# Carried scan states written two rounds ahead, and small preparation products asked for one round earlier, in a four-layer conv, scan and attention network

## The chip, the cores and the metric

The kernel runs on one core of one Trainium2 chip. The metric is the device time of one execution in microseconds; the median of three runs is given. One core has a matrix engine (TensorE, PE in the profile; PEld are its weight loads), three engines for elementwise work (VectorE or DVE, ScalarE or ACT, GpSimd or POOL), and a queue for transfers (SyncE or SP). Each engine has its own stream of instructions, and they wait for each other where data or a buffer asks for it.

## What is computed

The input is an image batch x of 4 x 56 x 56 x 96. Four layers follow each other: layers 0 and 1 are selective scans over the 3136 pixels of an image in four directions (rows and columns, each forwards and backwards), layers 2 and 3 are linear attention with a quantized feed-forward network. The change touches only the scans. For one direction, with 192 channels d and 16 states s per channel, the reference does this:

```
dt  = softplus(dt_raw @ dtw + dtb)            # per pixel and channel
d_a = exp(dt * a)                             # a = -exp(A_log), per channel and state
d_b = dt * b_ssm
h   = d_a * h + d_b * x_t                     # over the pixels, one after another
y_t = sum over s of h * c_ssm
```

dt_raw, b_ssm and c_ssm are small projections of the pixel's 192 channels. So each of the 192 x 16 = 3072 states per image and direction has a recurrence along 3136 pixels.

## The kernel before

**Tiling of the scan.** A direction of an image is cut into 7 chunks of 448 pixels. In a chunk the 3072 states are handled in 8 rounds (two halves e of the channels, four quarters q of the states), each with three groups g of 128 partitions. This gives 2 layers x 4 images x 4 directions x 7 chunks x 8 rounds = 1792 rounds; they are one long loop, `scans`, and everything else is woven into it.

**A round n.** The tile h has for each of the three groups 448 columns and two spare ones. It goes through these steps:

- `begin(n)`: TensorE spreads b over the partitions into the single PSUM buffer b (`spread_b`, L593), and GpSimd writes d_b * x for the third group into h (L686).
- `products(n)`: VectorE writes the same for the groups 0 and 1 (L691), reading b.
- `carried(n)`: ScalarE copies the states at the end of the chunk before (tile carry, 128x3) into the spare columns of h (L662), one per group, where the scan starts: columns 1, 451 and 901 in a forward direction, 450, 900 and 1350 in a reversed one. It is left out in the first chunk of a direction.
- `scan(n, g)`: VectorE runs the recurrence over group g (L698), reading the decays da[g] from PSUM.
- `decay(n + 1, g)`: ScalarE writes the decays of the next round into da[g] (L652), which has one buffer per group, so it follows `scan(n, g)`.
- `kept(n)`: ScalarE copies the states at the end of h into carry (L667).
- Last, GpSimd multiplies h with c into hc (L739); two rounds later TensorE sums hc over the states into y (`add_up`, L770), and every fourth time ScalarE moves y to SBUF (L777).

The tile h has three buffers. hc of round n is the last reader of h of round n.

**The order of the work is written out by hand.** The engines' streams follow the order of the Python program. In the loop over n it is: products(n); preparation of later chunks (`prepare`); slot F, where other work (the "lanes": projections, convolutions, layer norms and attention of other images) issues its ScalarE instructions; `prepare_on_scalar`; filler products that keep TensorE active (`keep_busy`, L757); begin(n + 1); add_up; the projections of a later chunk (`ahead`); scan and decay of group 0, carried(n + 1); slot C, where the lanes issue their TensorE instructions; scan and decay of groups 1 and 2; hc. `spend` books what the round's ScalarE and TensorE work costs, and the lanes may only issue what fits the rest; the filler is what is missing to a fixed amount.

**The preparation of a chunk** runs from 14 rounds before its first one. o counts its rounds, negative ahead of the chunk. In o = -12 and -11 TensorE projects the pixels into the single PSUM buffer pp (L433); in -10 ScalarE copies them to the tile cf (`rows`); then the rounding error of cf's bf16 half is kept in its lower rows, in two steps: `less` subtracts on TensorE (L586), ScalarE copies the rest (L573). Then `step_size` makes dt on TensorE (L479) for each half of the channels, into pp again, and `softplus` takes it from there on ScalarE (L489, L491). In -5 GpSimd forms dt * x (`times_u`, L504), and transfers spread both over the partitions.

Of the kernel before, what the change touches and what calls it, by code (L numbers as in the profile page):

```python
# [11 lines left out]
F32 = mybir.dt.float32  # L12
# [22 lines left out]
WIDE = NG * ROW + 2  # L35
# [131 lines left out]
class Net:  # L167
# [368 lines left out]
    def prepare(self, ch, o):  # L536

        nc = self.nc  # L540
        if o == -14:
            self.parameters(ch)
        elif o == -12:
            self.inputs(ch)
        elif o == -9:
            ch.cd = self.dram.tile([2 * NS, CS], F32, tag="cd", name="cd", bufs=3)
            nc.sync.dma_start(ch.cd, ch.cf[: 2 * NS])
            self.less(ch, 64)
        elif o == -8:
            self.less(ch, 96)  # L550
        elif o in (-7, -6):
            self.step_size(ch, o + 7)
        elif o == -5:
            self.times_u(ch)
            ch.dtd = self.park(ch.dtc)
        elif o == -4:
            ch.dud = self.park(ch.duc)
            self.spread_dt(ch, 0)
        elif o == -3:
            self.spread_du(ch, 0)  # L560
        elif o == 0:
            self.spread_du(ch, 1)
            self.spread_dt(ch, 1)
        if -3 <= o <= 0:
            self.fetch(ch, o + 3)

    def prepare_on_scalar(self, ch, o):

        if o == -10:
            self.rows(ch)  # L570
        elif o in (-9, -8):
            part = slice(64 if o == -9 else 96, 128)
            self.nc.scalar.copy(ch.cf[part], ch.ps[part])  # L573
        elif o in (-7, -6):
            self.softplus(ch, o + 7)

    def projected(self, ch, o):

        return () if o not in (-12, -11) else (o + 12,) if not ch.first else (0, 1) if o == -11 else ()
# [20 lines left out]
    def scans(self):  # L600

        nc, sp = self.nc, self.sp
        chunks = []
        for l in range(2):  # L610
            for i in range(NB):
                for n, (orient, rev) in enumerate(ORDER[l]):
                    for step in range(NCS):
                        ch = Step()
                        ch.l, ch.i, ch.orient, ch.rev, ch.step = l, i, orient, rev, step
                        ch.k = 2 * orient + rev if l == 0 else orient + 2 * rev
                        ch.c = NCS - 1 - step if rev else step
                        ch.n, ch.first = n, n == 0 and step == 0
                        ch.skip = n == 0
                        ch.last = n == 3 and step == NCS - 1  # L620
                        ch.cb, ch.dt, ch.du = [], [], []
                        chunks.append(ch)
        rounds = [(ch, e, q) for ch in chunks for e in range(NE) for q in range(NQ)]
        per = NE * NQ


        da = [self.psum.tile([128, 512], F32, name=f"da{g}")[:, : CS + 4] for g in range(NG)]
        for t in da:
            nc.vector.memset(t, 0.0)

        def steps(n):

            return [(ch, n - per * j) for j, ch in enumerate(chunks[max(0, n // per) : n // per + 3], max(0, n // per))]

        def ahead(n, project):
            for ch, o in steps(n):
                for e in self.projected(ch, o):
                    project(ch, e)

        for n in range(-14, 0):  # L640
            for ch, o in steps(n):
                self.prepare(ch, o)
            for ch, o in steps(n):
                self.prepare_on_scalar(ch, o)
            ahead(n, self.project_step)


        def decay(n, g):

            if n < len(rounds):  # L650
                ch, e, q = rounds[n]
                nc.scalar.activation(da[g][:, INNER], ch.dt[e][:, g], AF.Exp, scale=ch.par.na[:, e, q, g : g + 1])  # L652

        def column(t, at):

            return t[:, at : at + 2 * ROW + 1 : ROW]

        def carried(n):

            if n < len(rounds) and rounds[n][0].step:  # L660
                ch, e, q = rounds[n]
                nc.scalar.copy(column(hs[n], ROW if ch.rev else 1), ch.par.carry[:, e, q])  # L662

        def kept(n):
            ch, e, q = rounds[n]
            if ch.step < NCS - 1:
                nc.scalar.copy(ch.par.carry[:, e, q], column(hs[n], 2 if ch.rev else CS + 1))  # L667

        def own(n):
            ch, e, q = rounds[n]  # L670
            return NQ * e + q in (OWN_TAIL if ch.l and ch.i else OWN)

        hs, bs = {}, {}

        def tokens(t):

            return self.groups(t, 2)[:, :, :CS]

        def begin(n):

            if n < len(rounds):
                ch, e, q = rounds[n]
                bs[n] = self.spread_b(ch, q)
                hs[n] = sp.tile([128, WIDE], F32, name="h", bufs=3)
                if not own(n):
                    nc.gpsimd.tensor_tensor(tokens(hs[n])[:, 2], ch.du[e][:, 2], ch.cb[q][:, 1], ALU.mult)  # L686

        def products(n):
            ch, e, q = rounds[n]
            for g in range(3 if own(n) else 2):  # L690
                nc.vector.tensor_tensor(tokens(hs[n])[:, g], ch.du[e][:, g], bs[n], ALU.mult)  # L691

        def scan(n, g):
            ch, e, q = rounds[n]
            c = 1 if ch.step else 0
            way = slice(CS + 1 + c, 1, -1) if ch.rev else slice(2 - c, CS + 2)
            h = hs[n][:, g * ROW :]
            nc.vector.tensor_tensor_scan(h[:, way], da[g][:, way], h[:, way], 0.0, ALU.mult, ALU.add)  # L698

        begin(0)  # L700
        self.exp_and_ln()
        self.tables = True
        for g in range(NG):
            decay(0, g)
        late = []
        for n, (ch, e, q) in enumerate(rounds):
            r = NQ * e + q
            products(n)
            for c, o in steps(n):
                self.prepare(c, o)  # L710
            self.half_round()
            strided = [1.5 + 1.5 * ch.orient] * (r % NQ == 2)
            ahead(n, lambda c, _: strided.append(1.5 + 1.5 * c.orient))
            self.spend((0.6, 0.7, 1.7, 0, 0, 0, 0.7, 0.6)[r], (0.4, 1.3, 1.3, 0, 0, 0, 0, 0.4)[r] + sum(strided))
            yield "F", n, r
            for c, o in steps(n):
                self.prepare_on_scalar(c, o)
            ended = late.pop(0) if len(late) == 2 else None
            if ended:
                self.keep_busy(ended[2])  # L720
            begin(n + 1)
            if ended:
                self.add_up(*ended)
            ahead(n, self.project_step)
            self.half_round()
            for g in range(NG):
                if g == 1:
                    yield "C", n, r
                if g == 2 and ended and ended[2] == NQ - 1:
                    self.spend(0.6, 0)  # L730
                    self.keep_sums(*ended[:3])
                scan(n, g)
                if g == 2:
                    kept(n)
                decay(n + 1, g)
                if g == 0:
                    carried(n + 1)
            hc = sp.tile([128, NG, CS], F32, name="hc", bufs=3)
            nc.gpsimd.tensor_tensor(  # L739
                hc, tokens(hs[n]), ch.cb[q][:, 0].unsqueeze(1).to_broadcast([128, NG, CS]), ALU.mult,  # L740
            )
            late.append((ch, e, q, hc))
            del hs[n], bs[n]
        for ended in late:
            self.add_up(*ended)
        self.keep_sums(ch, e, q)
        yield "C", len(rounds), 0
# [619 lines left out]
```

## Time and profile before

| | |
|---|---|
| median of 3 runs | 8560.88 us (8560.84 to 8582.3) |
| profiled execution | span 8573.6 us, granted TensorE clock 0.892 |
| first and last hc (L739) | 115.8 us, 8187.3 us |
| copy of carried states (L662) | 1536 times, median 195 ns |
| subtraction product (L586) | 448 times, median 380 ns |
| dt product (L479) | 448, recorded as 896 passes, median 612 ns |
| filler products (L757) | 5061 times, 1410.0 us |

A page of the profile begins with each engine's busy time, its share of the span and its number of instructions. The groups that follow are instructions of one line: what they write and read, shape, count; then their busy time in us and the mean duration in ns; and last the idle time of the engine just before them, with what ended most of it. The table of waits gives for each pair the total in us, how often, and the longest. In the order of time a line begins with the start in us and the duration; "[idle before <-releaser]" tells how long the engine had stood, and for whom. Idle time counts only on the engine that sets the pace.

### The profile page before, as it was taken

The page shows a single profiled execution, that of the slowest core. Times are in us where ns is not written, and L with a number is a line of the kernel's source. Part 1 is how long each engine was busy: PE and PEld are TensorE (multiplying, and loading weights), DVE is VectorE, ACT ScalarE, POOL GpSimd, SP SyncE. Part 2 cuts the span into 40 slices and gives each one's busy share as a digit, 9 for nine tenths or more (in the row PEclk, how much of TensorE's full clock was granted, in tenths as well). Part 3 has the DMA queues.
Part 4 walks back from the last instruction along what each step waited for, and adds up shares of the span by engine and source line. Part 5 has one row for each costly group of instructions (what it writes and reads, how often), then busy time and mean ns, then how long its engine had stood idle before and what let it go on. Part 6 is the DMA issues. An engine that isn't in the chain of part 4 may idle for free. (4 is left out here: it accounts for less than half of the span.)

```text
span 8573.6 us, 119867 instructions
## 1 busy us (share of the span) xinstructions
PE 7605.2 (89%) x33851; PEld 2757.7 (32%) x33851; DVE 7521.8 (88%) x9555; ACT 6085.3 (71%) x12807; POOL 7185.1 (84%) x3991
## 2 busy tenths in 40 slices
PE   7888888898889888898889989998899888998997
PEld 3333322232323223232222323333333233333355
DVE  5999999989998999989899999999999999999931
ACT  5777777776777767776677766677766777767746
POOL 4898898988988988889889898898988888888820
PEclk8888889898998988989899989988999889998986
DMA  5776776667766676666767777666766667666621
GB/s 154 175 178 176 189 187 173 167 160 180 179 167 160 170 183 172 168 167 162 183 171 175 173 182 171 164 162 169 190 168 155 160 173 186 166 164 158 171 61 45
DMA packets 944162, 1417.81 MB, mean 165 GB/s; under 512 B 169410, under 2 KB 936644, under 8 KB 942628
## 3 DMA queue, kind: packets, MB, share of 16 engines
q1 hardware_dynamic: 942720, 1408.34, 66.6%
q8 instruction: 266, 4.36, 0.2%
q14 instruction: 404, 3.31, 0.1%
q10 hardware_dynamic: 772, 1.80, 0.1%
HBM read 1141.42 MB, written 268.14 MB: 164 GB/s over the span
## 5 line engine op out<-in xcount | busy, mean ns | idle before, releaser
L739 POOL TENSOR_TENSOR hc<-h,cb 128x1344 f32<-128x1344 f32 x1792 | 4883.2, 2725 | 826.4 <-DVE h L698 601.0
L698 DVE TENSOR_TENSOR_SCAN h<-da,h 128x449 f32<-128x449 f32 (+1 forms) x5376 | 5502.3, 1071 | 44.8 <-POOL h L686 37.8
L652 ACT ACTIVATE da<-dt,na 128x448 f32<-128x448 f32 x5376 | 3389.6, 633 | 820.3 <-DVE h L698 697.0
L691 DVE TENSOR_TENSOR h<-du,b 128x448 f32<-128x448 f32 x3584 | 2039.9, 606 | 516.4 <-ACT h L662 407.9
L770 PE MATMUL y<-hc,four 128*32 128x448 f32 x14336 | 1945.1, 618 | 7.1 <-POOL hc L739 7.1
L686 POOL TENSOR_TENSOR h<-du,cb 128x448 f32<-128x448 f32 x1792 | 1752.9, 978 | 103.7 <-DMA cb<-cd 96.6
L757 PE MATMUL y<-w,zeros 128*96 128x448 bf16 x5061 | 1410.0, 399 | 0.0
L593 PE MATMUL b<-cf,sel 128*128 128x448 bf16 x1792 | 680.4, 380 | 788.3 <-DVE h L691 782.0
L757 PEld LDWEIGHTS <-zeros 128*96 128x96 bf16 x5061 | 618.2, 135 | 1158.4 <-issue 1005.0
L662 ACT COPY h<-carry 128x3 f32<-128x3 f32 x1536 | 290.2, 189 | 630.1 <-POOL h L686 620.9
L770 PEld LDWEIGHTS y<-hc,four 128*32 128x32 f32 x14336 | 295.8, 113 | 1274.5 <-issue 877.0
L433 PE MATMUL pp<-U,wd 96*128 96x448 f32 x896 | 684.1, 853 | 7.3 <-DMA U<-u 4.3
L766 PE MATMUL y<-Y,ident 96*96 96x448 f32 x672 | 543.9, 899 | 13.5 <-ACT carry L667 5.3
L914 PE MATMUL ps<-win,dg 64*64 64x220 f32 (+9 forms) x1944 | 520.1, 469 | 0.0
L504 POOL TENSOR_TENSOR duc<-dtc,U 96x896 f32<-96x896 f32 x224 | 482.3, 2153 | 4.5 <-ACT dtc L491 4.5
L479 PE MATMUL pp<-cf,wd 12*96 12x448 f32 (+1 forms) x896 | 468.1, 603 | 16.1 <-ACT dtc L489 13.3
L667 ACT COPY carry<-h 128x3 f32<-128x3 f32 x1536 | 295.0, 192 | 175.6 <-DVE h L698 172.4
L573 ACT COPY cf<-pp 64x448 f32<-64x448 f32 x448 | 235.6, 526 | 180.8 <-PE pp L586 172.1
L777 ACT COPY Y<-y 96x448 f32<-96x448 f32 x448 | 341.0, 761 | 26.3 <-PE y L770 25.5
L489 ACT ACTIVATE dtc<-pp,wd 96x448 f32<-96x448 f32 x448 | 280.5, 626 | 107.6 <-PE pp L479 102.4
L914 PEld LDWEIGHTS ps<-win,dg 64*64 64x64 f32 (+2 forms) x1944 | 231.9, 163 | 334.9 <-issue 295.2
L593 PEld LDWEIGHTS <-sel 128*128 128x128 bf16 x1792 | 181.8, 101 | 417.4 <-issue 352.5
(432 smaller groups left out, 5970.0 us busy)
## 6 DMA issues: line engine op xcount, KB each, us to landing
cb<-cd SPq DMA_DIRECT2D x3584, 112.0 KB, 3.8
dt<-dd SPq DMA_DIRECT2D x1792, 168.0 KB, 4.3
du<-dd SPq DMA_DIRECT2D x1792, 168.0 KB, 4.1
dd<-dtc SPq DMA_DIRECT2D x224, 336.0 KB, 3.0
dd<-duc SPq DMA_DIRECT2D x224, 336.0 KB, 3.1
U<-u SPq DMA_DIRECT2D x112, 168.0 KB, 4.8
z<-w SPq DMA_DIRECT2D x56, 224.0 KB, 4.3
u<-w SPq DMA_DIRECT2D x56, 224.0 KB, 4.0
```

The lines of the kernel that those rows point to most:

```text
L433: self.nc.tensor.matmul(ch.ps.rearrange("p (a b) -> p a b", b=HS), ch.par.wx[:, e], self.in_order(self.U[e], ch.orient, ch.c * CS, CS), st ...
L504: self.nc.gpsimd.tensor_tensor(in_rows(ch.duc), in_rows(ch.dtc), u[:, :, lo : lo + CS // HS], ALU.mult)
L593: self.nc.tensor.matmul(ps, self.sel[:, q], self.upper(ch.cf), start=True, stop=True)
L652: nc.scalar.activation(da[g][:, INNER], ch.dt[e][:, g], AF.Exp, scale=ch.par.na[:, e, q, g : g + 1])
L686: nc.gpsimd.tensor_tensor(tokens(hs[n])[:, 2], ch.du[e][:, 2], ch.cb[q][:, 1], ALU.mult)
L691: nc.vector.tensor_tensor(tokens(hs[n])[:, g], ch.du[e][:, g], bs[n], ALU.mult)
L698: nc.vector.tensor_tensor_scan(h[:, way], da[g][:, way], h[:, way], 0.0, ALU.mult, ALU.add)
L739: nc.gpsimd.tensor_tensor(hc, tokens(hs[n]), ch.cb[q][:, 0].unsqueeze(1).to_broadcast([128, NG, CS]), ALU.mult,)
L757: self.nc.tensor.matmul(self.y[:C], self.zeros, self.some, start=False, stop=False)
L766: nc.tensor.matmul(o, w, self.in_order(a, ch.orient, ch.c * CS, CS), start=True, stop=False)
L770: nc.tensor.matmul(self.y[32 * n : 32 * n + 32], self.four, hc[:, g], start=n == 3, stop=n == 3 or q == NQ - 1,)
L914: self.nc.tensor.matmul(o[:, a - r0 : e - r0, x0:x1], diag[:, tap], win[:, a + dy - lo : e + dy - lo, x0 + dx : x1 + dx], start=n == 0, st ...
```

## The change

Two parts of the hand-written order are moved. First, the tile h of round n + 2 is taken, and the carried states are copied into it, at the end of round n, after the last decay; before, the tile of round n + 1 was taken in `begin(n + 1)` and the copy came after the first decay of round n + 1, in the middle of the scans. So VectorE's products and GpSimd's product into the same tile come after the copy instead of before it. Second, TensorE's `less` and `step_size` are asked for one round earlier, at the end of the round's TensorE work beside the projections, so that they can be done when ScalarE comes to read them in the next round. The bookings in `spend` are moved by a round to match. No arithmetic changes.

```diff
@@ prepare
         elif o == -9:
             ch.cd = self.dram.tile([2 * NS, CS], F32, tag="cd", name="cd", bufs=3)
             nc.sync.dma_start(ch.cd, ch.cf[: 2 * NS])
-            self.less(ch, 64)
-        elif o == -8:
-            self.less(ch, 96)
-        elif o in (-7, -6):
-            self.step_size(ch, o + 7)
         elif o == -5:
...
+    def on_tensor(self, ch, o):
+
+        for e in self.projected(ch, o):
+            self.project_step(ch, e)
+        if o in (-10, -9):
+            self.less(ch, 64 if o == -10 else 96)
+        elif o in (-8, -7):
+            self.step_size(ch, o + 8)
@@ scans
-        def ahead(n, project):
+        def ahead(n):
             for ch, o in steps(n):
-                for e in self.projected(ch, o):
-                    project(ch, e)
+                self.on_tensor(ch, o)
...
         def carried(n):
 
-            if n < len(rounds) and rounds[n][0].step:
+            if n < len(rounds):
                 ch, e, q = rounds[n]
+                hs[n] = sp.tile([128, WIDE], F32, name="h", bufs=3)
+                if not ch.step:
+                    return
                 nc.scalar.copy(column(hs[n], ROW if ch.rev else 1), ch.par.carry[:, e, q])
...
                 bs[n] = self.spread_b(ch, q)
-                hs[n] = sp.tile([128, WIDE], F32, name="h", bufs=3)
                 if not own(n):
...
+        carried(0)
+        carried(1)
         begin(0)
...
             strided = [1.5 + 1.5 * ch.orient] * (r % NQ == 2)
-            ahead(n, lambda c, _: strided.append(1.5 + 1.5 * c.orient))
-            self.spend((0.6, 0.7, 1.7, 0, 0, 0, 0.7, 0.6)[r], (0.4, 1.3, 1.3, 0, 0, 0, 0, 0.4)[r] + sum(strided))
+            strided += [1.5 + 1.5 * c.orient for c, o in steps(n) for _ in self.projected(c, o)]
+            self.spend((0.6, 0.7, 1.7, 0, 0, 0, 0.7, 0.6)[r], (1.3, 1.3, 0, 0, 0, 0, 0.4, 0.4)[r] + sum(strided))
...
             begin(n + 1)
             if ended:
                 self.add_up(*ended)
-            ahead(n, self.project_step)
+            ahead(n)
...
                 decay(n + 1, g)
-                if g == 0:
-                    carried(n + 1)
+            carried(n + 2)
             hc = sp.tile([128, NG, CS], F32, name="hc", bufs=3)
```

More of the change, by code (lines that the diff above doesn't have):

```diff
@@ L723, in scans @@
                 self.add_up(*ended)
-            ahead(n, self.project_step)
+            ahead(n)
             self.half_round()
```

## The prediction

> **What bounds the kernel.** I read the page's busy shares and costliest groups first, then the main loop alone (stretches), then who waits for whom, then the order of time around two waits.
>
> ```profile
> PE 7605.2 (89%) x33851; PEld 2757.7 (32%) x33851; DVE 7521.8 (88%) x9555; ACT 6085.3 (71%) x12807; POOL 7185.1 (84%) x3991
> ...
> L739 POOL TENSOR_TENSOR hc<-h,cb 128x1344 f32<-128x1344 f32 x1792 | 4883.2, 2725 | 826.4 <-DVE h L698 601.0
> L698 DVE TENSOR_TENSOR_SCAN h<-da,h 128x449 f32<-128x449 f32 (+1 forms) x5376 | 5502.3, 1071 | 44.8 <-POOL h L686 37.8
> ...
> L691 DVE TENSOR_TENSOR h<-du,b 128x448 f32<-128x448 f32 x3584 | 2039.9, 606 | 516.4 <-ACT h L662 407.9
> ...
> L686 POOL TENSOR_TENSOR h<-du,cb 128x448 f32<-128x448 f32 x1792 | 1752.9, 978 | 103.7 <-DMA cb<-cd 96.6
> ...
> L662 ACT COPY h<-carry 128x3 f32<-128x3 f32 x1536 | 290.2, 189 | 630.1 <-POOL h L686 620.9
> ```
>
> Three engines look almost equally full. Counts decide: 1792 rounds, each with three scans and two products on VectorE. In an undisturbed stretch (3001.7 to 3017.9 us in the order of time) a round starts every 4.01 us: 1.12 for both products and 3.05 for the scans, overlapping by 0.16, so VectorE is full. GpSimd needs 2.73 + 0.98 in such a round and then waits about 0.35 for the scan. The loop (first hc at 115.8 us, last at 8187.3) averages 8071.5 / 1791 = 4.51 us.
>
> ```profile
> 5100.00:5600.00 500.00, 478.88 (x2120) 174.40 (x2120) 463.24 (x588) 326.94 (x742) 441.86 (x250) 0.93 0.69 167
> ...
> 115.00:8190.00 8075.00, 7201.32 (x32192) 2513.00 (x32191) 7444.99 (x9362) 5834.76 (x12274) 7146.60 (x3947) 0.90 0.70 171
> ```
>
> Columns: length, then busy us and count of PE, PEld, DVE, ACT, POOL. In the loop VectorE idles 8075 - 7445 = 630 us, GpSimd 928, TensorE 874. VectorE is the bound, and its 630 us are all that any rearrangement can win.
>
> ```profile
> PE b L593 <- DVE h L691: 782.0, 693, 12.5
> ACT da L652 <- DVE h L698: 697.0, 1164, 3.8
> ACT h L662 <- POOL h L686: 620.9, 529, 7.0
> POOL hc L739 <- DVE h L698: 601.0, 882, 5.8
> DVE h L691 <- ACT h L662: 407.9, 337, 6.2
> ...
> ACT cf L573 <- PE pp L586: 172.1, 138, 4.0
> ...
> ACT dtc L489 <- PE pp L479: 102.4, 98, 6.2
> ```
>
> The other engines wait for VectorE; VectorE waits for the carried-state copy L662, 407.9 of its 630 us. This is the wait that the change aims at.
>
> **What the skill says.** The Trainium skill, Perfetto Trace Analysis, Sequencer Loop: an engine's instructions go into a queue and wait there for their semaphores, so a waiting L662 holds the decays behind it; the trace agrees (ACT idles 620.9 us at L662). Same page, Optimization Strategy: find the gaps of the saturated engine and make what ends them start sooner. ScalarE: Activation LUTs, What ACT_TABLE_LOAD costs: about 1283 ns for the load; the trace shows 1.28 us, and such pairs are one source of late ScalarE work. TensorE: Matmul & The Clock Gate, What's actually happening: the clock follows recent activity; the trace's granted clock is 0.90 in the loop, and its filler products (L757, 1410 us) are there for that, so a busy TensorE still holds slack.
>
> **Part 1: L662 and the h tile two rounds ahead.** No work is added or removed: 1536 copies of 0.19 us stay. What moves is their place. Today L662 of round n+1 stands behind the lanes' ScalarE work, the preparation's and the first decay. It delays VectorE in two ways, equal in size.
>
> Reversed directions (179 waits, 221 us, all at the second product). The copy's columns 450, 900, 1350 reach across GpSimd's third group (902 to 1349), so it comes after L686, which comes after hc and, once in eight rounds, after duc:
>
> ```profile
> 3024.64 2.53 POOL L504 TENSOR_TENSOR duc<-dtc,U 96x896 f32<-96x896 f32 x1
> ...
> 3026.52 0.62 DVE L691 TENSOR_TENSOR h<-du,b 128x448 f32<-128x448 f32 x1 [0.70 <-PE b L593]
> 3027.13 0.98 POOL L686 TENSOR_TENSOR h<-du,cb 128x448 f32<-128x448 f32 x1
> ...
> 3028.14 0.20 ACT L662 COPY h<-carry 128x3 f32<-128x3 f32 x1 [3.56 <-POOL h L686]
> ...
> 3028.37 0.62 DVE L691 TENSOR_TENSOR h<-du,b 128x448 f32<-128x448 f32 x1 [1.23 <-ACT h L662]
> ...
> 3028.91 3.05 DVE L698 TENSOR_TENSOR_SCAN h<-da,h 128x449 f32<-128x449 f32 x3
> ```
>
> Without the wait the second product starts at 3027.14, the first scan at 3027.7; the third scan, which alone needs L686 (done 3028.11), would start at 3029.7. Gain: 1.23 us.
>
> Forward directions (158 waits, 187 us, all at the first product). Here the columns 1, 451, 901 don't touch GpSimd's group; ScalarE is simply late:
>
> ```profile
> 3210.13 0.64 ACT L652 ACTIVATE da<-dt,na 128x448 f32<-128x448 f32 x1
> ...
> 3210.92 1.15 DVE L691 TENSOR_TENSOR h<-du,b 128x448 f32<-128x448 f32 x2 [1.32 <-ACT h L662]
> ...
> 3211.99 1.08 DVE L698 TENSOR_TENSOR_SCAN h<-da,h 128x449 f32<-128x449 f32 x1
> ```
>
> The products would run from 3209.6 to 3210.75, but the first scan also needs the decay, done at 3210.77: it starts at 3210.8, a gain of 1.15, not 1.32. A late decay caps the gain at the products' own time.
>
> I went through all 337 waits so: new start of the first scan = the later of (products begun without the wait, ended) and (first decay's end + 0.05); the old start less the new one is the gain. Sums: 162 us reversed, 130 us forward, **291 us** together; 143 of the 337 end at the decay. The remaining 117 us of the 408 stay as waits for decays.
>
> Kept at nothing, with what hides it: the new place is after decay(n+1, 2). There the copy waits for the third h buffer, which hc of round n-1 frees. In the trace that hc ends after decay(n+1, 2) in 60 rounds, 57 us in sum; behind the copy stand the lanes' ScalarE work and decay(n+2, 0), which can't start before the next first scan ends. By that moment (less 0.3 us) hc is still running in only 10 rounds. In reversed rounds L686 now waits for the copy instead: about 1 us after the scans' end against 2.9 for the hc ahead of L686.
>
> **Part 2: the small products a round earlier.** 448 of L586 (0.38 us) and 448 of L479 (two passes of 0.61) change place only. ScalarE's waits for them, 172.1 + 102.4 = 274.5 us, should nearly vanish. What is that worth to VectorE? In the 143 decay-capped cases such a wait lies ahead of the decay in 14, worth 5 us; ScalarE otherwise has slack (it waits 697 us for scans). I take **5 us**; upper end the 117 left over. The added waits: TensorE now stands for ScalarE's copy or exponential of the same round, with the lanes' matmuls and the next b (L593) behind it. b(n+1) is asked for as soon as the products of n are done and needed some 3 us later, so a wait under about 2 us is hidden; above that it becomes L691 <- PE b (66.7 us today). L593 alone waits 782 us, which is the slack that pays for it.
>
> The budget's shift also moves filler. None is written in the rounds two after a q of 0 (r = 2 and 6). The old charges that count are 0.4, 0.4, 1.3 (r = 7, 0, 1), the new ones 0.4, 1.3, 1.3: 0.9 x 1.6 = 1.4 fewer per chunk, about 320 of 5061, 0.28 us each (1410 / 5061): 90 us less TensorE time, off the path.
>
> **What takes the time back.** The lanes' work has to fit into shorter rounds. In the stretches 5100, 6100, 7100 and 7600 TensorE idles 21, 26, 32 and 35 us of 500, and the gains counted there are 17, 16, 20 and 18: I strike half of these 71, **35 us**. GpSimd: 928 idle less 291 leaves 637, no bound on average.
>
> Sum: 8560.9 - 291 - 5 + 35 = **8300 us**. After the loop (8190 to 8573) nothing changes.
>
> **Rivals.**
> - GpSimd and TensorE take over. In the example hc can start only 0.37 us earlier (GpSimd is full from 3024.64 to 3031.73), against 1.23 for VectorE. If the reversed gains shrink so, to 30% of 162 = 49: 130 + 49 - 35 = 144, 8417 us. For it: 386 rounds in which hc starts over 1 us after its scan. Against: VectorE may run ahead, since only its third scan needs L686 and the median slack there is 3.2 us.
> - All waits of L691 for L662 go and the decays come early enough: 8561 - 408 = 8153. Against: 143 late decays, which neither part moves much.
> - No change: the same rounds are stopped by decays, or b, at once: 8561.
> - Slower. TensorE waits 1 us at each of the second layer's 448 small products; its idle time from 4600 on is 300 us, so 148 spill over, and of the first layer's gain (153) half is kept: 8561 + 148 - 76 = 8633. For it: TensorE at 96% in the stretch shown, lanes' ScalarE bursts of 2 to 4 us. Against: the slack before b.
>
> **Chances.** Forecast 0.50, takeover 0.20, all waits 0.08, no change 0.07, slower 0.15. Faster by over 0.3% (below 8535): 0.78; within: 0.07; slower: 0.15. The range runs from the all-waits case, 8150, to 8570, just beyond no change; outside lie the slower case and some 0.04 below.
>
> **What would show it.** Right: L691 <- L662 and L662 <- L686 all but gone; VectorE's idle time in the loop near 350 us with decays (L698 <- ACT da) as the new cause, some 100 us; ACT <- PE pp down to a tenth; L739 <- DVE smaller. Wrong: L691 <- PE b well above 67 us, ScalarE standing at L662 for hc, or TensorE standing at L586 and L479 for cf and dtc by more than 300 us.

## The result and the profile after

The changed kernel takes 8360.38 us (median of 4 runs, 8352.0 to 8367.0) against 8563.33 us for the kernel before beside it (8560.84 to 8582.3): a ratio of 0.9758, with a 95% interval of 0.974 to 0.9775, 203 us or 2.4% faster. Forecast were 8300 us. The experiments ran on chips where the kernel before took 8569 to 8581 us, so below it is the ratios that are compared, each to the kernel before of its own chip.

The lines that answer to those of the prediction, first the page's engines and costliest groups (the scan is now L702, hc L744, the products L695, GpSimd's product L690, the copy of the carried states L667), then the loop alone:

```profile
PE 7469.6 (89%) x33633; PEld 2721.6 (33%) x33633; DVE 7516.6 (90%) x9555; ACT 6109.8 (73%) x12807; POOL 7177.3 (86%) x3991
...
L702 DVE TENSOR_TENSOR_SCAN h<-da,h 128x449 f32<-128x449 f32 (+1 forms) x5376 | 5507.1, 1071 | 134.9 <-ACT da L654 79.3
L744 POOL TENSOR_TENSOR hc<-h,cb 128x1344 f32<-128x1344 f32 x1792 | 4884.8, 2726 | 598.8 <-DVE h L702 413.6
...
L695 DVE TENSOR_TENSOR h<-du,b 128x448 f32<-128x448 f32 x3584 | 2019.6, 604 | 182.7 <-PE b L597 112.6
...
L667 ACT COPY h<-carry 128x3 f32<-128x3 f32 x1536 | 280.2, 182 | 66.3 <-POOL hc L744 63.5
```

```profile
116.00:7987.00 7871.00, 7072.48 (x31986) 2486.59 (x31988) 7440.39 (x9363) 5856.90 (x12267) 7136.88 (x3945) 0.91 0.71 176
```

The durations are those of before, to the nanosecond for the scan. What changed is the idle time. VectorE works 7440 us in the loop as it did, but idles 7871 - 7440 = 431 us instead of 630. In the last column of the products' row, 407.9 us for the carried states has become 112.6 us for b; in the scan's row, decays have come up with 79.3 us.

The table of waits of the changed kernel (total us, times, longest):

```profile
PE b L597 <- DVE h L695: 626.6, 609, 11.8
POOL hc L744 <- DVE h L702: 413.6, 624, 5.6
...
DVE h L695 <- PE b L597: 112.6, 143, 4.6
...
DVE h L702 <- ACT da L654: 79.3, 165, 2.1
...
ACT h L667 <- POOL hc L744: 63.5, 83, 3.0
...
ACT cf L568 <- PE pp L590: 57.7, 69, 2.4
...
ACT dtc L489 <- PE pp L479: 27.4, 34, 3.2
```

The carried-state waits are gone from it. ScalarE's waits for the small products, 274.5 us before, are 57.7 + 27.4 = 85. So both parts did what they were written for. But look at where TensorE now stands. These two rows are from the answer for the tile pp and TensorE's matmuls alone, in the list of what ended the idle time before an instruction on that tile (us, times). Of the changed kernel:

```profile
  ACT cf L568: 48.0, 50
  ACT dtc L489: 47.6, 29
```

And of the kernel before:

```profile
  ACT dtc L489: 13.3, 14
  ACT cf L573: 6.9, 13
```

The wait was turned round in part: ScalarE stood for TensorE 190 us longer before; now TensorE's matmuls stand for ScalarE 95.6 us at that tile instead of 20.2. Asked for all engines, the same answer gives 335 and 103 us, because it adds the idle time of the weight loads: these cover the same standing a second time (3.54 us beside the matmul's 2.74 in the case below), and time in which earlier matmuls still ran. The 201 and 134 us of an expectation below count in this way.

One such case in the order of time, in the second layer:

```profile
6572.04 0.96 PE L775 MATMUL y<-hc,four 128*32 128x448 f32 x8
...
6574.56 0.58 ACT L1206 ACTIVATE hq<-h 128x448 fp8e5<-128x448 f16 x1
6574.59 1.12 DVE L695 TENSOR_TENSOR h<-du,b 128x448 f32<-128x448 f32 x2
...
6575.16 0.53 ACT L568 COPY cf<-pp 32x448 f32<-32x448 f32 x1
...
6575.74 0.99 PE L479 MATMUL pp<-cf,wd 6*96 6x448 f32 x2 [2.74 <-ACT cf L568]
...
6576.65 1.13 PE L1223 MATMUL ps<-hq,w2q 128*96 128x448 fp8e5 x3
...
6579.34 0.57 PE L597 MATMUL b<-cf,sel 128*128 128x448 bf16 x1
...
6579.95 1.15 DVE L695 TENSOR_TENSOR h<-du,b 128x448 f32<-128x448 f32 x2 [0.64 <-PE b L597]
```

TensorE is done with add_up at 6573.0 and has the dt product next. That needs cf from L568, which sits on ScalarE behind a lane's run of quantizing steps until 6575.7. TensorE stands 2.74 us; behind it wait a lane's matmuls (L1223 and more), filler, and b. b comes at 6579.34, though the products that free its buffer ended at 6575.7, and VectorE stands 0.64 us for it. (The third of the lane's matmuls reads the hq of L1206, which was done at 6575.14, so a part of the standing would have come without the dt product too.) Before, the dt product came after the lane's matmuls.

The granted clock drops in this case too. Two stretches of the same trace, with length, busy us and count of PE, PEld, DVE, ACT and POOL, and then the granted clock:

```profile
6572.00:6576.00 4.00, 1.26 (x10) 0.40 (x10) 3.71 (x5) 3.85 (x8) 3.66 (x3) 1.00 1.03 247
6578.00:6580.00 2.00, 2.00 (x12) 1.27 (x16) 1.36 (x3) 1.97 (x4) 1.58 (x2) 0.50 0.00 0
```

The trace's record of the clock goes from 1.0 to 0.5 at 6576.93 and back at 6587.17. The b product took 0.57 us in this time and 0.36 us a round earlier, at 6571.75. In the loop TensorE stood for over 2 us at a small product 25 times, and 24 times the clock fell to 0.5 within 3.5 us of the end of the standing (2 of 2 in the kernel before).

The two layers show the result in sum. From the first hc to the last one of layer 0 the trace has 4013 us before and 3851 after; from there to the last hc of all, in layer 1, it has 4058 and 4017. Layer 0 gained 162 us, layer 1 only 41. In layer 1 VectorE lost 192 us of waits for the carried states and got 41 us more for b, 31 more in the lanes' work for TensorE, 17 more in that work for ScalarE, 39 more for decays and 16 more for GpSimd.

### The profile page after: what moved, and what is told of

It is laid out like the page before. It is cut to its first block, busy times and chain, and to the rows that moved or that the text cites. A ratio compares the mean times of both kernels' runs of the same rounds, so it can differ in the third digit from the quotient of the medians.

```text
span 8362.7 us, 119228 instructions
## 1 busy us (share of the span) xinstructions
PE 7469.6 (89%) x33633; PEld 2721.6 (33%) x33633; DVE 7516.6 (90%) x9555; ACT 6109.8 (73%) x12807; POOL 7177.3 (86%) x3991
## 5 line engine op out<-in xcount | busy, mean ns | idle before, releaser
L702 DVE TENSOR_TENSOR_SCAN h<-da,h 128x449 f32<-128x449 f32 (+1 forms) x5376 | 5507.1, 1071 | 134.9 <-ACT da L654 79.3
L744 POOL TENSOR_TENSOR hc<-h,cb 128x1344 f32<-128x1344 f32 x1792 | 4884.8, 2726 | 598.8 <-DVE h L702 413.6
L654 ACT ACTIVATE da<-dt,na 128x448 f32<-128x448 f32 x5376 | 3353.1, 632 | 1143.2 <-DVE h L702 1104.4
L695 DVE TENSOR_TENSOR h<-du,b 128x448 f32<-128x448 f32 x3584 | 2019.6, 604 | 182.7 <-PE b L597 112.6
L775 PE MATMUL y<-hc,four 128*32 128x448 f32 x14336 | 1913.0, 609 | 17.8 <-POOL hc L744 17.4
L690 POOL TENSOR_TENSOR h<-du,cb 128x448 f32<-128x448 f32 x1792 | 1754.1, 979 | 141.4 <-DMA cb<-cd 110.1
L762 PE MATMUL y<-w,zeros 128*96 128x448 bf16 x4843 | 1354.0, 397 | 0.0
L775 PEld LDWEIGHTS y<-hc,four 128*32 128x32 f32 x14336 | 294.2, 113 | 1182.5 <-issue 660.5
L433 PE MATMUL pp<-U,wd 96*128 96x448 f32 x896 | 664.5, 830 | 12.1 <-DMA U<-u 8.3
L919 PE MATMUL ps<-win,dg 64*64 64x220 f32 (+11 forms) x1998 | 547.3, 471 | 0.0
L479 PE MATMUL pp<-cf,wd 12*96 12x448 f32 (+1 forms) x896 | 476.2, 613 | 71.7 <-ACT dtc L489 47.6
L667 ACT COPY h<-carry 128x3 f32<-128x3 f32 x1536 | 280.2, 182 | 66.3 <-POOL hc L744 63.5
L489 ACT ACTIVATE dtc<-pp,wd 96x448 f32<-96x448 f32 x448 | 281.7, 629 | 31.3 <-PE pp L479 27.4
L827 PEld LDWEIGHTS ps<-avg,w 96*112 96x112 f32 (+2 forms) x1944 | 249.9, 193 | 108.1 <-issue 59.0
```

The lines of the kernel that those rows point to most:

```text
L433: self.nc.tensor.matmul(ch.ps.rearrange("p (a b) -> p a b", b=HS), ch.par.wx[:, e], self.in_order(self.U[e], ch.orient, ch.c * CS, CS), st ...
L744: nc.gpsimd.tensor_tensor(hc, tokens(hs[n]), ch.cb[q][:, 0].unsqueeze(1).to_broadcast([128, NG, CS]), ALU.mult,)
L762: self.nc.tensor.matmul(self.y[:C], self.zeros, self.some, start=False, stop=False)
L775: nc.tensor.matmul(self.y[32 * n : 32 * n + 32], self.four, hc[:, g], start=n == 3, stop=n == 3 or q == NQ - 1,)
L919: self.nc.tensor.matmul(o[:, a - r0 : e - r0, x0:x1], diag[:, tap], win[:, a + dy - lo : e + dy - lo, x0 + dx : x1 + dx], start=n == 0, st ...
```

## Experiments

**Each part alone.** The first is the kernel before with the tile and the copy moved, the second with the products and their bookings moved.

```diff
 # part 1 alone (begin and carried as in the change)
...
-                if g == 0:
-                    carried(n + 1)
+            carried(n + 2)          # takes the h tile as well
 # part 2 alone
-            self.less(ch, 64)       # and the others in prepare
...
+            ahead(n)                # on_tensor: projections, less, step_size
```

> The kernel before with only the carried states and the h tile moved two rounds ahead. Theory A (the carried states' wait was the whole gain): 8360 to 8400 us, the waits of VectorE's products for the copy gone as in the changed kernel. Theory B (part 2 makes TensorE stand for ScalarE and gives gain back in the second layer): 8300 to 8330 us, faster than the changed kernel, with products waiting less than 80 us for b. Theory C (both parts are needed, since ScalarE still stands for TensorE's small products): above 8430 us, with decays late.

Measured: 8304.2 us, ratio 0.9681 (0.9663 to 0.9699). That is faster than the changed kernel. Theory A's time is missed, B's is met.

> The kernel before with only the small products of the preparation asked for a round earlier, and their bookings. Theory A: 8540 to 8570 us, within 0.3% of before; ScalarE's waits for these products fall from 274 us to under 100, and VectorE's wait for the carried states stays near 400 us. Theory B: 8590 to 8630 us, slower, with products waiting over 100 us for b. Theory C: 8450 to 8500 us.

Measured: 8612.13 us, ratio 1.0043 (1.0027 to 1.0059): slower. The time is theory B's, its sign isn't: the products' wait for b was 70.3 us, hardly above the 66.7 of before. What rose in the loop is the waiting of the lanes' VectorE work for TensorE, from 70 to 104 us. ScalarE's wait for cf's subtraction fell to 62.4 us, VectorE's for the carried states stayed at 403.0. Of part 1 alone, the table of waits:

```profile
ACT cf L573 <- PE pp L586: 165.9, 126, 4.0
...
ACT dtc L489 <- PE pp L479: 107.5, 99, 5.9
...
DVE h L700 <- ACT da L652: 81.6, 166, 2.7
...
DVE h L693 <- PE b L593: 69.2, 111, 4.1
ACT h L665 <- POOL hc L742: 68.1, 94, 3.0
```

ScalarE stands for the small products as long as in the kernel before (273 us), and it costs nothing visible: the scans wait for decays 81.6 us with it and 79.3 without. What part 2 took away was idle time of an engine with slack; what it put in shows most in the wait for b, 69.2 us here and 112.6 in the changed kernel. Part 1 alone has layer 0 in 3838 us and layer 1 in 3968: against the changed kernel, 13 and 49 us less.

**Moved products or moved bookings?** The changed kernel once more, and three between it and part 1 alone.

> The changed kernel itself, to stand beside the others on one chip: a ratio of 0.974 to 0.978 to before.

Measured: 0.9732 (0.9714 to 0.975), just below what was expected and lower than its first 0.9758; so two kernels with medians 0.25% apart are not told apart by one comparison.

```diff
 # part 1 with the bookings of the changed kernel
-(0.4, 1.3, 1.3, 0, 0, 0, 0, 0.4)[r]
+(1.3, 1.3, 0, 0, 0, 0, 0.4, 0.4)[r]
```

> Part 1 alone with the bookings of the changed kernel, the small products staying where they were. Theory W (part 2 costs because TensorE stands for ScalarE at the small products): as part 1 alone, ratio 0.966 to 0.970. Theory K (the shifted bookings put the lanes' work and the filler at worse places): as the changed kernel, 0.974 to 0.978.

Measured: 0.9678 (0.9661 to 0.9695), as part 1 alone.

> The changed kernel with the bookings of before. Theory W: as the changed kernel, ratio 0.974 to 0.978, with TensorE standing over 250 us for cf and dtc at the small products. Theory K: as part 1 alone, 0.966 to 0.970.

Its edit is the same line the other way. Measured: 0.9759 (0.9742 to 0.9777), as the changed kernel. TensorE's matmuls stand 94 us for cf and dtc; with the weight loads counted in it is 328, and only so over the expected 250. These runs are of one chip, and together they put theory K aside: the bookings are not the cost, the moved products are.

```diff
 # subtractions moved, dt products at their old place in prepare
+        elif o in (-7, -6):
+            self.step_size(ch, o + 7)
...
-        elif o in (-8, -7):         # in on_tensor
-            self.step_size(ch, o + 8)
```

> Part 1 with only the subtraction products moved (and their bookings), the dt products at their old place. In the changed kernel TensorE stands 201 us for dtc and 134 us for cf at the tile pp (61 and 42 before). If the dt products carry the cost (the second one now waits for the exponential of the same round, since pp has one buffer), the ratio is 0.967 to 0.970; if the subtractions carry it, 0.973 to 0.977; if both, 0.970 to 0.973.

Measured: 0.9703 (0.9685 to 0.9721). (The 201 and 134 us are counts with the weight loads; the changed kernel's matmuls alone stand 47.6 and 48.0.) The middle suggests that both kinds of products carry some; the interval reaches into those of both neighbours, so the shares stay open.

**Standing, or only a later turn for the lanes?** In the changed kernel two things happen at the new place: TensorE stands for ScalarE, and the lanes' matmuls come later by the products' own length. Filler in that place, which waits for nothing, was to separate them.

```diff
             ahead(n, self.project_step)
+            extra = (4, 0, 0, 4, 0, 0, 1, 1)[r] if ended else 0
+            self.add_zeros(extra)
+            self.work += extra      # so many fewer in the next keep_busy
```

> Part 1 alone with the bookings of the changed kernel, the small products at their old place, and at the changed kernel's new place ahead of the lanes' matmuls filler of about the same length (1 in rounds 6 and 7, 4 in rounds 0 and 3; so many fewer in the next round's filler). The filler waits for nothing of ScalarE's. Theory W (it is the standing for ScalarE that costs): ratio 0.966 to 0.970, as without the filler. Theory D (it is enough that the lanes' matmuls come later by the products' length): 0.972 to 0.976, as the changed kernel.

Measured: 0.9793 (0.978 to 0.9807), slower than the changed kernel. This looks like theory D, but the kernel isn't a clean test. One of its two fours stands in round 3, where the changed kernel has no moved product: its second dt product is in round 1. And filler was left over. Its row on the page against the changed kernel's, which has the same bookings:

```profile
L763 PE MATMUL y<-w,zeros 128*96 128x448 bf16 x5846 | 1705.4, 398 | 0.0
```

```profile
L762 PE MATMUL y<-w,zeros 128*96 128x448 bf16 x4843 | 1354.0, 397 | 0.0
```

1003 fillers more were left over, since many rounds had none to give up, and with them 350 us of TensorE time. The wait for b rose to 115.7 us. So work ahead of the lanes' matmuls can cost as much without any standing.

The traces tell the two apart for the wait for b. The table sorts it (us) by what TensorE did since the b product before, and by the granted clock when the wait ended:

| products' wait for b | part 1, new bookings | changed | changed, second time | with filler there |
|---|---|---|---|---|
| in all | 82.1 | 112.6 | 100.5 | 115.7 |
| TensorE had stood at a small product | 0.5 | 21.8 | 18.7 | 0 |
| a small product, but no standing | 39.2 | 48.0 | 40.6 | 47.7 |
| no small product | 42.3 | 42.8 | 41.3 | 68.0 |
| ended at full clock | 59.2 | 58.2 | 60.2 | 99.4 |
| ended at half clock | 22.9 | 54.4 | 40.3 | 16.4 |

What part 2 adds comes mostly in rounds in which TensorE stood, and wholly at half clock; what the filler adds comes at full clock. So in the wait for b, the later turn alone doesn't explain part 2. No run separates the standing from the clock. And b isn't all: from the first hc to the last VectorE idles 428 us in the changed kernel and 376 with part 1 and the new bookings. Of these 52 us some 30 are b's; the rest, spread over smaller waits, stays open.

**Is TensorE too full?** The prediction charged 35 us for a full TensorE in the second layer.

```diff
-            self.add_zeros(int(max(0.0, WARM - self.work) + 0.5))
+            self.add_zeros(int(max(0.0, (WARM, 4.8)[l] - self.work) + 0.5))
```

> The changed kernel with the filler's aim lowered from 6.8 to 4.8 in the second layer's rounds, about 700 to 900 fillers fewer of 2143 there. If a full TensorE is what took back most of the second layer's gain (theory T), the second layer gets 40 to 80 us shorter than 4017 us and the waits of products for b and of lanes' VectorE work for TensorE fall from 146 us by half. Rival: the granted clock falls with less activity, and TensorE is as late as before or later: second layer 4010 to 4080 us. Rival: TensorE is late since it stands for ScalarE at the small products: no change in the second layer, within 10 us.

Measured: 0.9738 (0.972 to 0.9756), as the changed kernel; layer 1 took 4027 us, with 840 fillers fewer. (The profiled execution took 8378.8 us, the median of the five is 8352.11.) Theory T's gain did not come: the two waits in layer 1 that were to halve went from 146 to 160 us. The granted clock over layer 1 fell from 0.91 to 0.87, and VectorE's wait for b in the whole loop stayed (104.4 us). The two rivals foretold much the same time and aren't told apart by it.

**b ahead of the filler**, on the changed kernel and on part 1 alone:

```diff
+            begin(n + 1)
             if ended:
                 self.keep_busy(ended[2])
-            begin(n + 1)
-            if ended:
                 self.add_up(*ended)
```

> The changed kernel with b of the next round asked for ahead of the filler products instead of behind them. If VectorE's new largest wait (113 us for b) comes from filler standing ahead of b on a late TensorE, it falls under 60 us and the time by 30 to 50 us, to 8310 to 8330. If TensorE is late because of the work of the lanes as a whole, the wait falls little; and since the filler no longer runs while b waits for VectorE (627 us), it then pushes everything behind it: 8370 to 8420 us.

Measured: 0.9714 (0.9699 to 0.973), 8333.45 us. From its table of waits:

```profile
PE b L597 <- DVE h L695: 835.4, 829, 12.6
...
DVE h L702 <- ACT da L654: 109.6, 197, 2.1
...
DVE h L695 <- PE b L597: 57.9, 84, 5.3
```

The wait for b halves as expected, and 30 us more of waits for decays take a good part back. The time is some 0.4% below the first reading of the changed kernel (0.9758), as forecast, but against the second (0.9732) the gain is within the noise.

> Part 1 alone with b of the next round asked for ahead of the filler. In the changed kernel the same edit took the wait for b from 113 to 58 us and the time by some 0.3%. If that wait is still worth time here (69 us), the ratio is 0.963 to 0.967, the fastest of all; if TensorE without the standing is early enough, 0.967 to 0.970.

Measured: 0.9712 (0.9698 to 0.9725), outside both forecasts: not faster than part 1 alone but, as far as the intervals tell, slower. VectorE waits for b only 48.9 us, but for decays 98.6. The pair is telling: with b ahead of the filler, the kernel with part 2 and the one without have the same ratio, 0.9714 and 0.9712, so no cost of part 2 is left that is clear of noise. This fits a cost that comes where b stands behind the filler, late in TensorE's queue. But the edit also shortens the standing itself, from 95.6 to 62.4 us of the matmuls for cf and dtc, and makes part 1 alone slower, so the place of b isn't shown to be the reason.

**The two causes behind the old wait.** The prediction split it into GpSimd's product (reversed directions) and ScalarE's lateness (forward).

```diff
+            carried(n + 1)          # tile and copy, still behind ScalarE's other work
             begin(n + 1)
...
-                if g == 0:
-                    carried(n + 1)
```

> The kernel before with the h tile and the carried states of round n + 1 only moved ahead of GpSimd's product in the same round, so still behind the lanes' and the preparation's ScalarE work but ahead of the first decay; part 2 left out. It frees the reversed directions of the wait for GpSimd and leaves ScalarE's lateness in both. Theory of the prediction (two separate causes, 162 us reversed and 130 us forward): the reversed part comes, the forward one comes only as far as the first decay stood ahead of the copy: 8580 less 130 to 220, ratio 0.975 to 0.985. Rival (ScalarE's lateness is all that counts, GpSimd's product was a bystander): 0.993 to 1.000. Rival (one round is enough): 0.966 to 0.970.

Measured: 0.9736 (0.9722 to 0.975), 8339.84 us, some 230 us off, just past the upper end of what was expected. What is left of the wait, and a new one of GpSimd's product, which now comes after the copy:

```profile
DVE h L693 <- ACT h L665: 143.1, 185, 5.2
POOL h L688 <- ACT h L665: 127.4, 115, 4.1
```

So 265 of the 408 us fall when the copy only passes GpSimd's product and the first decay; the second round of distance takes away the remaining 143 and is worth some 0.5% more (0.9681). By directions, the trace is 178 us shorter in the reversed ones, all that part 1 alone gives there (180), and 62 us in the forward ones, where part 1 alone gives 83. GpSimd was no bystander, and one round is not enough.

**Four h buffers on part 1 alone** (bufs=4 instead of 3):

> Part 1 alone with four h buffers instead of three. ScalarE's new wait for GpSimd's last reader of h (68 us in 94 waits) goes to zero. If that wait is hidden, as the prediction had it: ratio 0.966 to 0.970, as part 1 alone. If it delays decays (82 us of scans' waits for them): 0.960 to 0.964.

Measured: 0.9684 (0.9669 to 0.97), as with three. The wait for hc, 68.1 us with three, is gone, and the time is the same: it was hidden.

## Why the prediction came out as it did

The direction, part 1's mechanism and the range held; the gain, 203 us against 261, was forecast too large by 58.

- **What bounds the kernel:** right. Every kernel here has VectorE busy some 7440 us in the loop, and the differences are its idle time.
- **Part 1, 291 us less 35:** right in size, in part because errors cancel. Alone it gave 8581.3 - 8304.2 = 277 us against 256. By layers, 175 and 90 us, where the event count had 153 and 138 before the 35. By directions the trace gives 180 us reversed and 83 forward, against 162 and 130: freeing GpSimd was worth more than counted, passing ScalarE's lateness less. (By the prediction's own rule its forward example gains 1.17 us, not 1.15.)
- **Its hidden terms:** right. The wait for the third h buffer was 63.5 us in 83 waits (57 in 60 rounds had been read off) and cost nothing with or without a fourth buffer. Decays were forecast as the next cause with some 100 us and are 79.3. ScalarE's waits for the small products were to fall to a tenth and fell to a third.
- **Part 2, a gain of 5 us:** this is the step that failed. It costs 0.0043 of the time by itself. In the changed kernel it costs the distance from 0.9678 to 0.9732, measured on one chip, or from 0.9681 to 0.9758, on two: 46 to 66 us of 8561. The gain's half of the step was right: ScalarE's standing was worth nothing. What failed is that the added waits of TensorE were put at nothing in the sum. The prediction said itself that a wait above some 2 us reaches VectorE through b, but took b's slack to pay for all of them; no such wait was priced. The trace has 25 stands of over 2 us, with the clock at half after 24 of them, and in the example the lanes' matmuls and filler still come between the standing and b. The prediction named two signs of this. L695 waiting for b well above 67 us is there, 112.6. TensorE standing over 300 us for cf and dtc is there only if the weight loads are counted in (335); the matmuls stand 95.6.
- **The 35 us for a full TensorE:** the place was right, the second layer, the mechanism not supported: fewer fillers there bought nothing. Part 1 alone did fall 48 us short of the count in that layer (90 against 138); why stays open.
- **VectorE's idle time near 350 us:** 431 measured. With part 1 alone the trace gives 166 in layer 0 and 210 in layer 1, 376 together: so 55 of the 81 us too many are again part 2's.
- **Filler, 320 fewer:** 218 fewer (5061 to 4843), and no matter: with old or new bookings the time is the same.

The fastest kernels are those with part 1 alone: 0.9681, 0.9678 with the new bookings and 0.9684 with four buffers, which the intervals don't tell apart. They beat both the kernel before and the changed one.

## What to carry to other kernels

Moving a tiny copy two rounds earlier won more than 3%, because the saturated engine waited for it, while it stood behind a product of one engine and in the queue of another that ran late. Go through the saturated engine's waits one by one, and credit each only up to the next thing that would have stopped it. Asking for a product earlier so that a slack engine need not wait was worth nothing here, and it turned part of the wait round onto an engine whose queue does feed the saturated one. Before such waits are counted as hidden, the longest ones need a price: here 25 were of over 2 us. Where one edit has two parts, run each alone: here one hid a loss of a fifth of the other's gain.

## What the runs showed of the hardware that was not expected

A short standing of TensorE was enough to be followed by half clock. In the changed kernel the clock fell from 1.0 to 0.5 within 3.5 us after 24 of the 25 stands of over 2 us at the small products, and after 6 of the 12 of 1 to 2 us that began at full clock. A stretch at 0.5 lasted 5.7 us on average.

TensorE's busy time hardly followed the amount of filler. With 840 fillers fewer the filler's own row fell by 191.5 us, from 1354.0 to 1162.5, but TensorE's busy time only from 7469.6 to 7441.5: the mean granted clock went from 0.898 to 0.878, and the y products (L775) took 620 ns instead of 609. With the same number of fillers as in the changed kernel, but placed behind b instead of ahead of it, the clock rose to 0.923 and the y products took 597 ns.
